# Four graph layers on one core: the order of the first graphs, the place of the exact arm, and the costs of a list planner

## The chip, the core and the metric

The kernel runs on one core of a Trainium2 chip. The metric is the device time of one execution in microseconds; lower is better. The engines are called as in the profile: PE (TensorE's matmuls, with PEld for its weight loads), DVE (VectorE), ACT (ScalarE), POOL (GpSimd) and SP (SyncE, which here issues all the DMAs).

## The reference, cut to what matters

The input is 32 graphs of 512 nodes with 128 features each, and one 512 x 512 matrix `adj` that all graphs share. Four layers follow one another; each normalizes, applies ReLU, and adds its result to x.

```python
h = relu(layernorm(x)); x = x + L0(h, adj)   # messages weighted by sigmoid scores
h = relu(layernorm(x)); x = x + L1(h, adj)   # five GRU steps
h = relu(layernorm(x)); x = x + L2(h, adj)   # adj @ (h @ weight) + bias
h = relu(layernorm(x)); x = x + L3(h, adj)   # Chebyshev sum, powers 0 to 3 of adj

# L0
x_h = elu(h @ Wi + bi)
e = sigmoid(a_tgt[:, :, None] + a_src[:, None, :] + be)      # a_src, a_tgt = x_h @ We, two halves
e = e * (adj + 0.005 * (1 - (adj != 0)))
recv = elu(concat([e @ x_h, x_h * e.sum(-1, keepdims=True)]) @ Wn + bn)
out = concat([recv, x_h]) @ Wm + bm

# L1, five times
m = adj @ h                                                  # both matrices are adj here
z = sigmoid(concat([m, m]) @ w3.T + h @ u3.T + biases)
r = sigmoid(concat([m, m]) @ w4.T + h @ u3.T + biases)
c = tanh(concat([m, m]) @ w5.T + (r * h) @ u5.T + biases)
h = (1 - z) * h + z * c
```

Here `adj` holds only zeros and ones, which matters for the kernel: a 0/1 matrix is unchanged when it is rounded to the one-pass matmul format.

## The kernel before, in words

**Staging.** The graphs go in groups of four. A graph's x is 512 x 128, kept on chip as 128 partitions x 512 columns. Nearly every operation works on one such 128x512 tile. A full fp32 product of that size takes TensorE several passes. A product with `adj` takes one pass for each part: when the matrix is exact in the one-pass format, the other operand is split into a high and a low part (`parts`, ACT L739 and DVE L743), and two one-pass products give the result (L769 in layers 1 and 2, L859 in layer 3). So the program has two arms: the exact one, and one with full fp32 products. A test of `adj` decides at run time: DVE L472 compares each rounded part with the original and sums the differences, PE L479 adds up over the partitions, DVE L484 writes the integer `inexact`, and each engine loads it (L906) and branches (L907). With this input the exact arm runs. Before the change the exact arm is the `else` of the branch, so the other arm's instructions stand between the branch and it.

**A list planner.** The instruction order is not written by hand. The kernel's Python lists operations with `op(engine, us, due, emit, reads, writes, ...)`: an assumed duration, a due time, and what it reads and writes. `Plan.order` then runs a list schedule: at each event, each engine takes of its ready operations the one that is due first, if its buffers are free. `result` is the assumed delay until others can use what was written; `known` computes it for a reader. Operations marked `two` (DVE with two operands in SBUF) and all POOL operations are not planned at the same time (`shared`). The order that comes out is emitted as it is, and every engine executes its own queue in that order. On the chip an engine starts an instruction when its semaphores allow, whatever the plan thought; what the plan fixes is the order.

The plan has two stretches: what is planned before `BRANCH` (30 us of planned time) comes ahead of the branch for both arms, and the rest is planned once for each arm. The due times come from `begin(b)`: graphs start `PACE` (56 us) apart, the first ones `FIRST_PACE` (10 us) apart, the last ones `LAST_PACE` apart.

**The first graphs.** Before the branch, SP loads graph 0, `Wi`, the four row blocks of `adj` (`A_nat`), small weights, then graphs 1 to 3. PE transposes graph 0's normalized tile (L334) and `adj` (L464, 16 transposes into four PSUM buffers). ACT rounds the transposed `adj` to `A_r` (L466) and scales it (L468); DVE makes the score mask (L469) and the test (L472). Then layer 0 of graph 0 goes on: the `Wi` product (L405), elu (ACT L492, L410, L495, DVE L497, L499), the product with `W_tok` for messages and scores (L521), the spread of the target scores (L558), tanh (ACT L572), masking (DVE L575), aggregation (PE L583).

**Later graphs.** In layer 0 of graphs 4 to 31, the target scores go through DRAM: a small tile is written (`d`) and read back as one row spread to all partitions (L548, `f<-d`), and the sums over the four score tiles are made on POOL (L594, three additions a graph). POOL also takes the power for each normalization (L439) and adds two biases to x (L414). In layer 1 every step writes h to DRAM and reads it back transposed (`m<-f`, `f<-m`). DVE has the adds and the gate combinations (L794, L801, L811 to L815) and block transposes (L346).

**Buffers.** There are 36 `f` tiles, 8 PSUM banks `b`, 8 small `s` tiles, and a few of other kinds; a planned operation that writes a new value waits in the plan until one is free.

Of the kernel before, what the change touches and what calls it, by code (L numbers as in the profile page):

```python
# [38 lines left out]
class Plan:  # L39
# [7 lines left out]
    def __init__(self, slots, ahead, last):  # L47
# [3 lines left out]
        self.shared, self.now = 0.0, 0.0  # L51

    def op(self, eng, us, due, emit, reads=(), writes=(), two=False, keep=0, result=None):
# [4 lines left out]
        o = Op(eng, us, self.RESULT[eng] if result is None else result, emit, two, keep)  # L58
        for v in reads:
            o.before.add(v.writer)  # L60
# [37 lines left out]
    def known(self, o, to):  # L98

        own = {"PE": 0.0, "ACT": 0.13, "DVE": 0.13}  # L100
        return o.known - o.result + own[o.eng] if to.eng == o.eng in own else o.known

    def order(self, end=None):
# [9 lines left out]
        for i, o in enumerate(left):  # L113
            index[o] = i
            o.waits = sum(not b.begun for b in o.before)
            o.ready = max([0.0, *(self.known(b, o) for b in o.before if b.begun)])
# [19 lines left out]
        while events:  # L136
# [3 lines left out]
            for e in self.until:  # L140
# [12 lines left out]
                for x in passed:  # L153
                    heapq.heappush(ready[e], x)
                if o is None:
                    continue
# [29 lines left out]
def tile_four_graph_layers(  # L186
# [35 lines left out]
    PACE, FIRST_PACE, LAST_PACE = 56.0, 10.0, 30.0  # L222
    BRANCH = 30.0
# [44 lines left out]
    op("DVE", 0.2, -9, lambda: nc.vector.memset(at(ones), 1.0), [], [ones])  # L268
    op("POOL", 0.2, -9, lambda: nc.gpsimd.memset(at(neg_half), -0.5), [], [neg_half])
# [8 lines left out]
    def load(v, src, due, us=0.5, to=None):  # L278
        op("SP", us, due, lambda: nc.sync.dma_start(at(v) if to is None else to(at(v)), src), [], [v])
        return v  # L280

    def load_const(src, shape, name, due, us=0.5):
        return load(const(name, shape), src, due, us)
# [10 lines left out]
    def load_graph(b, due):  # L294
        op("SP", 1.5, due, lambda: nc.sync.dma_start(
# [3 lines left out]
    load_graph(0, -9)  # L299
    Wi_sb = load_const(Wi, [P, P], "Wi_sb", -9)  # L300
    A_nat = [Val("f") for _ in range(NC)]
    for ic in range(NC):
        load(A_nat[ic], adj[ts(ic, P), :], -8, 1.3)
    bi_sb = load_column(bi, "bi_sb", -8)
# [6 lines left out]
    load_graph(1, -6)  # L311
# [3 lines left out]
    bm_bc = load_const(bm.partition_broadcast(P), [P, P], "bm_bc", -5)  # L315
    load_graph(2, -4)
    load_graph(3, -3)
# [107 lines left out]
    def layernorm(b, due):  # L425
# [13 lines left out]
        op("POOL", 1.2, due, lambda: nc.gpsimd.tensor_tensor(  # L439
# [19 lines left out]
    n_odd = const("n_odd", [P, NC])  # L459
    for jc in range(NC):  # L460
        pt, z, odd = Val("b"), Val("f"), Val("f")
# [3 lines left out]
        op("PE", T_TR, jc, turn, [*A_nat, ident], [pt])  # L465
# [480 lines left out]
```

## Time and profile before

| | |
|---|---|
| median of 3 runs | 1702.48 us (1700.79 to 1705.91) |
| the profiled execution's own time | 1704.23 us |
| its span, first to last instruction | 1702.4 us |
| mean granted TensorE clock | 0.996 |
| busy PE, DVE, ACT, POOL | 1665.6, 1478.8, 1099.6, 377.3 us |

The profile shows one execution. Busy time of PE is the union of its records, whose ends are modelled: dense matmuls overlap in it. The views used are the page (busy times, groups of instructions by line), the stretches (busy time of each engine in a window, with the granted clock), the timeline (instructions in order of time, neighbours of one kind merged, with the idle time before them and what ended it), the waits (who waited for whom in total), and the chain of waits that ended last. "issue" stands where the profile shows no reason for a wait.

### The profile page before, as it was taken

To read this page: it belongs to the slowest core of one execution; us is meant where nothing else is said; L and a number is where in the kernel's file an instruction comes from. 1 tells how busy PE (TensorE), PEld (TensorE's weight loads), DVE (VectorE), ACT (ScalarE), POOL (GpSimd) and SP (SyncE) were. 2 spreads that over 40 slices of the span, in tenths; PEclk is the share of its full clock that TensorE was granted. 3 is DMA by queue.
4 is the path that set the end of the run, shared out by engine and by line. 5 is a ranking of instruction groups with operands and counts; after the bars stand their busy time and mean duration, and the time that the engine had idled before them with its cause. 6 is when DMAs were issued, how large, how long until landed. Compare 5 with 4: busy or idle time off the path is not lost.

```text
span 1702.4 us, 21136 instructions
## 1 busy us (share of the span) xinstructions
PE 1665.6 (98%) x6521; PEld 1065.7 (63%) x6521; DVE 1478.8 (87%) x3325; ACT 1099.6 (65%) x2075; POOL 377.3 (22%) x301
## 2 busy tenths in 40 slices
PE   5999999999999999999999999999999999999998
PEld 3565555666666666665666665666666666666787
DVE  5789999999989998889989898899999888877842
ACT  5786767777666776566676666667576756655550
POOL 3231122312312222222212222122232221001210
PEclk8999999999999999999999999999999999999999
DMA  3122323253333332242333333333333323222302
GB/s 95 36 69 93 123 96 99 70 150 92 93 99 112 100 105 88 76 123 93 94 108 91 94 107 87 100 107 107 89 112 95 95 86 101 81 75 75 95 6 62
DMA packets 266873, 156.54 MB, mean 92 GB/s; under 512 B 75392, under 2 KB 235008, under 8 KB 266752
## 3 DMA queue, kind: packets, MB, share of 16 engines
q1 hardware_dynamic: 266752, 155.12, 30.9%
q8 instruction: 53, 0.87, 0.2%
q14 instruction: 68, 0.56, 0.1%
HBM read 82.25 MB, written 72.81 MB: 91 GB/s over the span
## 4 chain that ended last, share of the span: by engine, by line
PE 84%; DVE 8%; DMA 3%; ACT 3%; issue 2%; SPq 0%; POOL 0%; DVEq 0%; ACTq 0%; POOLq 0%
PE b L405 39%; PE b L769 18%; PE b L859 9%; PE b L850 6%; PE b L583 4%; PE b L619 3%; DMA f<-d 2%; PE b L521 2%; DVE f L575 2%; PE b L833 1%; DVE r L743 1%; PE b L606 1%; ACT f L447 1%; DVE f L794 1%; DVE f L346 1%
## 5 line engine op out<-in xcount | busy, mean ns | idle before, releaser
L394 ACT COPY f<-b 128x512 f32<-128x512 f32 x360 | 207.8, 585 | 151.6 <-PE b L769 105.8
L769 PE MATMUL b<-AQ,r 128*128 128x512 f32 x1024 | 304.4, 439 | 0.8 <-DVE r L743 0.8
L439 POOL TENSOR_TENSOR s<-s,nhalf 128x4 f32<-128x4 f32 x128 | 156.0, 1219 | 645.8 <-DVE s L437 610.1
L769 PEld LDWEIGHTS b<-AQ,r 128*128 128x128 f32 x1024 | 192.1, 188 | 90.5 <-issue 49.9
L794 DVE TENSOR_TENSOR f<-f,b 128x512 f32<-128x512 f32 x320 | 211.8, 677 | 20.4 <-PE b L405 16.5
L447 ACT ACTIVATE f<-x,s 128x128 f32<-128x128 f32 x512 | 210.1, 488 | 23.0 <-DVE s L442 22.7
L346 DVE STREAM_TRANSPOSE f<-f 128x512 f32<-128x512 f32 x244 | 204.6, 845 | 22.3 <-ACT f L447 21.7
L859 PE MATMUL b<-r,A_r 128*128 128x512 f32 x768 | 223.6, 426 | 0.0
L410 ACT ACTIVATE f<-f,b4w 128x512 f32<-128x512 f32 x160 | 115.4, 723 | 165.2 <-DVE f L794 164.7
L594 POOL TENSOR_TENSOR f<-f,f 128x512 f32<-128x512 f32 x84 | 130.9, 1559 | 307.3 <-DVE f L575 231.0
L405 PE MATMUL b<-f,u5T 128*128 128x512 f32 x320 | 163.9, 596 | 7.9 <-DVE f L801 7.8
L859 PEld LDWEIGHTS b<-r,A_r 128*128 128x128 f32 x768 | 139.0, 189 | 44.9 <-issue 23.0
L405 PE MATMUL b<-f,w4T 128*128 128x512 f32 x320 | 163.4, 593 | 0.2 <-ACT f L394 0.2
L405 PE MATMUL b<-f,u3T 128*128 128x512 f32 x320 | 163.0, 592 | 0.4 <-DMA f<-m 0.4
L405 PE MATMUL b<-f,w5T 128*128 128x512 f32 x320 | 162.8, 592 | 0.0
L405 PE MATMUL b<-f,w3T 128*128 128x512 f32 x320 | 162.5, 592 | 0.0
L769 PE MATMUL b<-A_r,r 128*128 128x512 f32 x512 | 151.8, 439 | 2.5 <-DVE r L743 2.5
L410 ACT ACTIVATE f<-b,b5w 128x512 f32<-128x512 f32 x160 | 109.2, 684 | 64.5 <-PE b L405 63.5
L743 DVE TENSOR_TENSOR r<-f,r 128x512 fp32r<-128x512 f32 x192 | 143.1, 749 | 8.2 <-ACT r L739 8.1
L850 PEld LDWEIGHTS b<-V,f 128*128 128x128 f32 x1024 | 130.5, 192 | 24.8 <-issue 20.6
L410 ACT ACTIVATE f<-f,b3w 128x512 f32<-128x512 f32 x160 | 115.2, 720 | 42.5 <-DVE f L794 41.6
L811 DVE TENSOR_TENSOR f<-f,f 128x512 f32<-128x512 f32 x160 | 114.7, 718 | 29.3 <-ACT f L410 28.7
(103 smaller groups left out, 2623.8 us busy)
## 6 DMA issues: line engine op xcount, KB each, us to landing
m<-f SPq DMA_DIRECT2D x244, 256.0 KB, 2.1
f<-m SPq DMA_DIRECT2D x184, 256.0 KB, 2.9
f<-m SPq DMA_DIRECT2D x240, 64.0 KB, 2.2
x<-in_x_dram SPq DMA_DIRECT2D x32, 256.0 KB, 3.1
out_dram<-x SPq DMA_DIRECT2D x32, 256.0 KB, 2.4
f<-d SPq DMA_DIRECT2D x28, 256.0 KB, 5.1
f<-in_adj_dram SPq DMA_DIRECT2D x4, 256.0 KB, 4.0
f<-in_L_gnn_weight_dram SPq DMA_DIRECT2D x2, 224.0 KB, 3.3
```

What stands on the lines that cost most here:

```text
L346: op("DVE", us, due, lambda: nc.vector.transpose(view_out(at(blocks)), view_in(at(src))), [src], [blocks])
L394: op("ACT", us, due, lambda: nc.scalar.copy(at(t), at(src)), [src], [t])
L405: nc.tensor.matmul(to, at(w), of, start=start, stop=stop)
L410: op("ACT", us, due, lambda: nc.scalar.activation(at(dst), at(src), AF.Tanh, bias=at(bias), scale=scale), [src, bias], [dst])
L439: op("POOL", 1.2, due, lambda: nc.gpsimd.tensor_tensor(stat(SCALE), stat(VAR), at(neg_half), op=ALU.pow), [s, neg_half], [s])
L447: nc.scalar.activation(at(h)[:, ts(c, P)], at(X[b])[:, c, :], AF.Relu, bias=stat(SHIFT)[:, c : c + 1], scale=stat(SCALE)[:, c : c + 1],)
L594: op("POOL", 1.4, d - 10, lambda: nc.gpsimd.tensor_tensor(at(dst), at(a), at(c), op=ALU.add), [a, c], [dst])
L743: op("DVE", T_VEC, due, lambda: nc.vector.tensor_tensor(part(lo), whole(), part(hi).bitcast(F32), op=ALU.subtract), [src, hi], [lo], two=two)
L769: nc.tensor.matmul(at(pa), at(part)[:, ts(jc, P)], view(at(columns)[:, jc, :]), start=jc == n == 0, stop=jc == NC - 1 and n == PARTS - 1,)
L794: op("DVE", T_VEC, d, lambda: nc.vector.tensor_tensor(at(s), at(u), at(pg), op=ALU.add), [u, pg], [s])
L850: nc.tensor.matmul(at(pz)[:, ts(i, D)], at(hT[i])[:, ts(ic, P)], at(V[k]), start=i == 0, stop=last and i == G - 1,)
L859: nc.tensor.matmul(at(pz), at(adjT)[:, jc, ts(ic, P)], at(part), start=False, stop=jc == NC - 1 and n == PARTS - 1,)
```

## The change

There are five edits.

1. *Loads.* Graph 1 is loaded right behind graph 0, `bi` ahead of `adj`, graph 2 right behind `adj`; `bm_bc` not before `BRANCH`. The planned cost of these issues goes from 1.5 and 1.3 us to 0.65.
2. *Test and preparation of `adj`.* The rounding for the test is made on the untransposed blocks (a new ACT copy into `short`, and the DVE comparison reads two SBUF tiles), so the test doesn't wait for the transposes. The transposes and `A_r` get later due times (8 and 22).
3. *Arms.* The condition is turned round, so that the exact arm follows the branch directly and the other arm stands behind it.
4. *Planner.* `BRANCH` 30 to 18, `FIRST_PACE` 10 to 14. Assumed costs: POOL power 1.2 to 1.35, POOL addition 1.4 to 1.6, the row read's result 3.6 to 5.0. In the arms, what another engine writes counts as known to PE 0.3 us later (`slack`). Before the branch, an operation is held when one with an earlier due time is about to be ready, and a planned operation may carry an earliest time.
5. *Dummies.* Ahead of the branch, wherever the plan leaves PE without work, it puts a matmul of `ones` with `ones` (128 x 128, planned at 0.224 us) into a PSUM bank that is set aside for it (`spare`) until the branch. There are 53 of them in the listing: 31 ahead of everything else, then 3, 15, 1 and 3 between the first operations.

```diff
+        if to.eng == o.eng in own:
+            return o.known - o.result + own[o.eng]
+        return o.known + (self.slack if to.eng == "PE" else 0.0)
...
+                if o is not None and end is not None and any(
+                    c.due < o.due and t < now + 0.3 * o.us for t, _, c in coming[e]
+                ):
+                    heapq.heappush(ready[e], (o.due, index[o], o))
+                    o = None
+                if o is None and e == "PE" and end is not None and self.idle.known <= now:
+                    order.append(self.idle)
+                    self.until[e] = now + self.idle.us
...
-    PACE, FIRST_PACE, LAST_PACE = 56.0, 10.0, 30.0
-    BRANCH = 30.0
+    PACE, FIRST_PACE, LAST_PACE = 56.0, 14.0, 30.0
+    BRANCH = 18.0
...
+    spare = places["b"].pop()
+    plan.free["b"].pop()
+    plan.idle = Op("PE", 0.224, 0.0, lambda: nc.tensor.matmul(
+        spare[:, :P], at(ones), at(ones), start=True, stop=True), False, 0)
+    plan.idle.known = 0.4
...
     load_graph(0, -9)
+    load_graph(1, -9)
     Wi_sb = load_const(Wi, [P, P], "Wi_sb", -9)
+    bi_sb = load_column(bi, "bi_sb", -9)
...
-        load(A_nat[ic], adj[ts(ic, P), :], -8, 1.3)
-    bi_sb = load_column(bi, "bi_sb", -8)
+        load(A_nat[ic], adj[ts(ic, P), :], -8, 0.65)
+    load_graph(2, -8)
...
-    bm_bc = load_const(bm.partition_broadcast(P), [P, P], "bm_bc", -5)
-    load_graph(2, -4)
-    load_graph(3, -3)
+    bm_bc = load_const(bm.partition_broadcast(P), [P, P], "bm_bc", -5, earliest=BRANCH)
+    load_graph(3, -6)
...
-        op("POOL", 1.2, due, lambda: nc.gpsimd.tensor_tensor(
+        op("POOL", 1.35, due, lambda: nc.gpsimd.tensor_tensor(
...
+    for ic in range(NC):
+        short, odd = Val("q"), Val("f")
+        op("ACT", T_COPY, 9, lambda ic=ic, short=short: nc.scalar.copy(
+            at(short), at(A_nat[ic])), [A_nat[ic]], [short])
+        op("DVE", 0.7, 9, lambda ic=ic, short=short, odd=odd: nc.vector.scalar_tensor_tensor(
+            at(odd), at(short).bitcast(F32), 1.0, at(A_nat[ic]),
+            op0=ALU.mult, op1=ALU.not_equal, accum_out=at(n_odd)[:, ic : ic + 1]),
+            [short, A_nat[ic]], [odd, n_odd], two=True)
...
-            op("SP", T_DMA, d, read, [row], [tgt], keep=KEEP, result=3.6)
+            op("SP", T_DMA, d, read, [row], [tgt], keep=KEEP, result=5.0)
...
-                op("POOL", 1.4, d - 10, lambda: nc.gpsimd.tensor_tensor(
+                op("POOL", 1.6, d - 10, lambda: nc.gpsimd.tensor_tensor(
...
+            plan.slack = 0.3
+            plan.free["b"].append((BRANCH, len(places["b"]) - 1))
...
-    with tc.If(taken > 0) as branch:
+    with tc.If(taken < 1) as branch:
+        arm(True)
+    with branch.Else():
         arm(False)
-    with branch.Else():
-        arm(True)
```

In the changed file the lines have moved: L394 becomes L417, L405 L428, L439 L462, L464 L495, L521 L548, L583 L610, L594 L621, L743 L773, L769 L799, L801 L831, L859 L889. The new lines that the steps name are L485 (ACT copy of `A_nat`), L487 (DVE test), L499 (ACT scaling of the transposed `adj`, before L468) and L288 (the dummies).

## The prediction

> **What bounds the kernel now.** I read the busy shares first, then the stretches of the first 50 us, then the waits of TensorE and the timeline around its longest ones. The first line says that TensorE (PE) is the bound and that little over 2% of the span can come back at all.
>
> ```profile
> PE 1665.6 (98%) x6521; PEld 1065.7 (63%) x6521; DVE 1478.8 (87%) x3325; ACT 1099.6 (65%) x2075; POOL 377.3 (22%) x301
> ```
>
> Busy PE is not yet work, since each record's end is modelled. So I price the records by their distance from start to start where the chain of waits shows them dense: 0.429 us for a 128x512 f32 record ("L405 x10" in 4.29), 0.2285 for a one-pass 128x512 (L769 and L859, 3.64 for 16 and 6.36 for 28), 0.112 for a 128-column f32 record (L850 x48 in 5.36), 0.109 for a transpose. With the counts of the groups: 2016 x 0.4288 + 2364 x 0.2285 + 2048 x 0.112 + 85 x 0.109 = 864.5 + 540.2 + 229.0 + 9.3 = 1643 us. The span is 1702.4, so 59.3 us are not work. Placed by start time, 27.1 of them lie in the first 50 us, 27.3 between 50 and 1650, and 4.9 at the end, where nearly all come after the last matmul (an addition, a store of 2.4 us to landing, the closing barrier).
>
> The first 50 us, by stretches (us, then busy us and records of PE, PEld, DVE, ACT, POOL, the granted clock, DMA):
>
> ```profile
> 0.00:10.00 10.00, 3.11 (x12) 2.50 (x13) 1.65 (x11) 4.31 (x9) 2.49 (x12) 1.00 0.69 194
> 10.00:20.00 10.00, 3.14 (x12) 2.06 (x10) 8.71 (x39) 5.47 (x10) 3.82 (x4) 0.80 0.19 55
> 20.00:30.00 10.00, 8.25 (x29) 5.08 (x30) 4.95 (x13) 7.63 (x18) 3.60 (x3) 0.52 0.16 47
> 30.00:40.00 10.00, 7.84 (x28) 4.03 (x27) 3.70 (x15) 5.33 (x12) 2.42 (x4) 1.00 0.43 108
> 40.00:50.00 10.00, 8.95 (x38) 5.25 (x37) 8.46 (x27) 8.99 (x22) 3.99 (x7) 1.00 0.00 0
> ...
> 8.31 3.62 PE L464 MATMUL b<-ident,f 128*128 128x128 f32 x16
> 20.61 2.10 PE L521 MATMUL b<-W_tok,f 128*128 128x130 f32 x8 [7.46 <-DVE f L499]
> 34.22 1.12 PE L583 MATMUL b<-f,f 128*128 128x512 f32 x2 [2.16 <-DVE f L499]
> ```
>
> Between 13 and 20 us DVE is full and PE waits 7.46 us for the first elu (DVE L499 of the file before); from 20 to 30 PE works at half clock. Then comes the branch. Here every engine jumps, because the exact arm is the second:
>
> ```profile
> L907 SPq COMPARE_BRANCH  x1: 45/45/45, 24.4 to 24.4; - x1
> L907 PEldq COMPARE_BRANCH  x1: 4549/4549/4549, 29.6 to 29.6; - x1
> ...
> 32.39 0.69 DVE L497 SCALAR_TENSOR_TENSOR f<-f,f 128x512 f32<-128x512 f32 x1 [4.03 <-issue]
> 33.05 0.40 POOL L751 CAST swap<-ident 128x128 fp32r<-128x128 f32 x1 [2.72 <-issue]
> ```
>
> SP's next instruction comes at 27.10, 2.7 us after its branch; PE's branch lasts 4.55 us, of which queued matmuls hide all but the 2.16 above. From 34.22 on PE is nearly full.
>
> In the middle PE waits for DVE, in a few pieces of over a microsecond:
>
> ```profile
> PE b L405 <- DVE f L801: 7.8, 7, 1.9
> PE b L769 <- DVE r L743: 3.3, 2, 2.5
> ...
> 1049.98 3.26 POOL L594 TENSOR_TENSOR f<-f,f 128x512 f32<-128x512 f32 x2 [0.69 <-DVE f L575]
> 1050.36 1.75 DVE L743 TENSOR_TENSOR r<-f,r 128x512 fp32r<-128x512 f32 x1
> 1052.04 1.76 DVE L815 SCALAR_TENSOR_TENSOR f<-f,f 128x512 f32<-128x512 f32 x1
> ...
> L594 POOL TENSOR_TENSOR f<-f,f 128x512 f32<-128x512 f32 x84 | 130.9, 1559 | 307.3 <-DVE f L575 231.0
> f<-d SPq DMA_DIRECT2D x28, 256.0 KB, 5.1
> ```
>
> The timeline shows a cause: while POOL adds (L594), a DVE instruction with two SBUF operands takes 1.75 us, not 0.685, and 5 us later PE loses 1.9 us on L801. In the whole trace 57 such instructions run over 1.0 us, 48 of them over an L594, and their excess is 53.5 us. The planner keeps the two apart but with 1.4 us for an addition that takes 1.56, and 3.6 for a row read that takes 5.1. From 50 to 1650 the waits whose end I can name cost PE about 15 us of the 27.3; the rest is handover between forms.
>
> **The change, part by part.** By the listings of the instructions, the exact arm has the same PE work as before (1643.1 us at the prices above) plus 53 dummy matmuls ahead of the branch. So everything is waits.
>
> *Start.* SP's queue now begins x0, x1, Wi, bi, then adj: the adj parts move back by two issues (0.95 us), to land at about 6.7 to 8.4 instead of 5.6 to 7.5 (issue to landing 4.0). PE meanwhile runs 31 dummies of 0.223 us from about 1.1. While the clock is half each takes 0.446. The change from half to full came 5.6 us after PE's first work in this trace (at 12.5; transposes at 0.213 each before it, 0.109 later), so I take 5 us: 11 dummies cold, 20 warm, end at 10.6 (9.7 to 11.4). That is 2 us after adj has landed, but it hides ACT's four new copies of A_nat (L485, 4 x 0.59) of which two stand ahead of x0's normalization, and DVE's test (4 x 0.69), which moves to plain adj. Then 16 transposes at 0.109 and x0's 4: 12.8; the copy L417 (0.59), three dummies; Wi (0.86) ends at 14.3; ACT's three scalings of the transposed adj (L499 of the changed file) are done at 14.9, then Exp, Tanh, Relu at 0.65 each to 16.9; DVE's two follow to 17.7. W_tok starts at 17.75 instead of 20.61. The last test, the count and the two masks of DVE bring `inexact` at about 20 instead of 23.5; graph 1's Wi comes at 21.2 instead of 26.33, graph 0's first aggregation (L610) at 23.2 instead of 28.20. The DMAs behind the branch (bm_bc, x4, then the weights) start at about 21 instead of 27; POOL's x + bm now waits for bm_bc there, and only the residual add much later reads it. By 23.2 PE has done 5.8 us of work: lost 17.4. Before, when PE was full at 34.22, 24.8 were lost, and 2.3 more by 50. With the same 2.3 after: 19.7 against 27.1, **7.5 us less** (4 to 10).
>
> *Branch.* Part of that 7.5 is 2.16 us of PE idle that goes if falling through is cheap. The trace shows no branch not taken. Bounds: 0.05 us (the instruction's own 45 ns on SP, ACT, POOL) and again 2.7 to 4.5. I take the low end, since the listed next instruction follows in line; the other end costs 1.5 to 2.3 us. The price comes back at the end: each engine now jumps over the other arm. SP's jump (2.7) starts after its last issue and lies beside the landing of 3.0; DVE's, if as long as its gap of 4.03, ends 0.5 us after the barrier did. I take **+0.5** (0 to 1.5). [...] The rows show 2.7 to 4.5, so I use them.
>
> *Clock.* [...] Here 16 transposes, with a piece of Wi behind them, filled the time before the grant at 12.5, so I charge nothing.
>
> *Costs in the list.* L594 at 1.6, L439 at 1.35 (measured 1.22, median 1.38), the row read at 5.0, 0.3 of slack for what PE reads, first graphs at 14 apart instead of 10. No instruction is added; the orders of all queues change. Bounds: nothing of the 15 us, all of it, or, with new collisions, a loss. PE now loses 15 for 53.5 us of stretching. If the right L594 price removes some two thirds (a POOL chain of three additions now slips by 3 x 0.16), PE gets about **9 us** back. I take that (-5 to +14).
>
> *Tail.* By the listing 95.9 us of PE work stand behind the last u5T product, 95.0 before, and no PE gaps lie there today: 0. SP's stores keep their order.
>
> Sum: -7.5 - 9 + 0.5 = -16. The profiled execution took 1704.23 (span 1702.4 and 1.8 around it), 1.75 above the median of the runs; I put the 16 to the median 1702.5: **1686.5 us**. About 0.3%, 5 us, is what can be told from no change.
>
> **Rivals.** *The middle keeps its waits:* the collisions only move, because POOL starts when DVE hands it data and not when planned. For it: L594 mostly waits for L575. Time: 1702.5 - 7 = 1695.5. *The start doesn't gain:* the dummies run cold to 14.9 (31 x 0.446) and the not-taken branch costs as much as the taken one. Against: the grant after 5.6 us. Time: -1 - 9 + 0.5: 1693. *The order is not what PE waited for in either place:* no change, 1702. *Slower:* in the middle, DVE at 93 to 99% from 150 to 450 us falls behind by new collisions. At 0.29 us of PE for each us stretched, it decides from 24 us more stretching (some 26 collisions) on, where the start's 7 us are gone; with 45 more, 1708. Against: POOL is given 84 x 0.2 + 128 x 0.15 = 36 us more room.
>
> **How the numbers follow.** The sum as told, 1678 to 1692: 0.60. Waits stay, to 1698: 0.20. Start fails, 1690 to 1698: 0.08. More than told, below 1678: 0.05. No change: 0.04. Slower: 0.03. The range 1677 to 1697 leaves out under 2 in 10.
>
> **What would show it.** Right: `inexact` near 20 us, the DVE and PE gaps at the branch gone, the full clock before 10 us and kept, PE full from about 24, lost work at 50 us near 20; stretched DVE instructions down from 57 to about 20, L801's waits below 3 us. Wrong: a half clock after 12 us, a gap of 2 us or more behind the branch, 50 or more stretched instructions, PE gaps after 1600, or an end more than 6 us after the last matmul.

## The result, and the profile after

The changed kernel takes 1696.03 us (median of 6 runs, 1693.68 to 1697.62) against 1703.74 for the kernel before (6 runs, 1700.79 to 1705.97): a ratio of 0.9954, with a 95% interval of 0.9943 to 0.9966. That is 7.7 us less. The forecast was 16 less; the time lies inside its range (1677 to 1697), but only just.

The profiled execution of the changed kernel took 1695.31 us, with a span of 1693.5. By the prediction's prices its PE work is again 1643.1 us (the dummies are not counted), so 50.4 us of the span are not work, against 59.3. By place, with PE's records sorted by their start ("middle" is from 50 to 1600 us in all that follows):

| not work, us | 0 to 50 | 50 to 1600 | 1600 to the end |
|---|---|---|---|
| before | 27.1 | 27.0 | 5.2 |
| after | 15.9 | 27.0 | 7.5 |
| step of the sum | -7.5 | -9 | +0.5 |
| measured | -11.2 | 0.0 | +2.3 |

So the start brought more than forecast, the end cost more, and the whole error is the middle. The lines of the page that answer to those shown of before (busy engines, the group of POOL's additions, the row read):

```profile
PE 1671.6 (99%) x6627; PEld 1075.1 (63%) x6627; DVE 1484.5 (88%) x3325; ACT 1100.3 (65%) x2079; POOL 381.7 (23%) x301
...
L621 POOL TENSOR_TENSOR f<-f,f 128x512 f32<-128x512 f32 x84 | 131.4, 1565 | 230.1 <-DVE f L602 159.2
...
f<-d SPq DMA_DIRECT2D x28, 256.0 KB, 5.4
```

PE is fuller on paper, but its 106 records more (6627 against 6521) are the two records of each of the 53 dummies. POOL's additions and the row read last about as long as before (1565 ns against 1559, 5.4 us against 5.1); only the planner's opinion of them changed.

The stretches of the first 50 us of the kernel after, and the start in its timeline:

```profile
0.00:10.00 10.00, 8.96 (x64) 8.96 (x65) 3.99 (x25) 4.86 (x10) 3.23 (x11) 1.00 0.76 226
10.00:20.00 10.00, 10.00 (x91) 9.37 (x89) 8.00 (x32) 8.31 (x18) 2.22 (x4) 1.00 0.08 20
20.00:30.00 10.00, 9.36 (x34) 4.67 (x33) 8.02 (x26) 9.02 (x21) 6.73 (x10) 1.00 0.55 150
30.00:40.00 10.00, 10.00 (x33) 5.08 (x32) 6.95 (x19) 10.00 (x24) 3.35 (x3) 1.00 0.01 3
...
1.04 8.97 PE L288 MATMUL b<-ones 128*128 128x128 f32 x62 [1.04 <-DVE ones L283]
9.85 1.47 PE L495 MATMUL b<-ident,f 128*128 128x128 f32 x12
16.91 1.06 PE L548 MATMUL b<-W_tok,f 128*128 128x130 f32 x8
18.77 0.14 DVE L511 CAST inexact<-b 1x1 int32<-1x1 f32 x1
21.70 3.70 PE L610 MATMUL b<-f,f 128*128 128x512 f32 x8 [0.64 <-DVE f L602]
```

The column of the granted clock is 1.00 in every stretch, where before had 0.80 and 0.52. It leaves out the time ahead of the first grant: until 4.81 us a dummy's record takes 0.213 us from start to start, behind it 0.112. The 7.46 us wait ahead of W_tok is filled, and 0.64 us is all that PE waits behind the branch. From 22 us on PE is full.

PE's longest waits in the kernel after:

```profile
PE b L799 <- DVE r L773: 4.5, 3, 2.5
PE b L428 <- DVE f L831: 3.1, 7, 0.8
PE b L428 <- ACT f L417: 2.5, 4, 1.1
```

The 7.8 us of before's L801 (now L831) are down to 3.1, as hoped; the split of the operands (L773) has 4.5 instead of 3.3, and ACT's copies (L417, before L394) have 2.5 instead of 1.4. Two-operand DVE instructions of over 1.0 us number 65 instead of 57, and their excess is 64.0 us instead of 53.5.

### The profile page after: what moved, and what is told of

Read it like the earlier page. It is cut to its first block, busy times and chain, and to the rows that moved or that the text cites. A ratio compares the mean times of both kernels' runs of the same rounds, so it can differ in the third digit from the quotient of the medians.

```text
span 1693.5 us, 21347 instructions
## 1 busy us (share of the span) xinstructions
PE 1671.6 (99%) x6627; PEld 1075.1 (63%) x6627; DVE 1484.5 (88%) x3325; ACT 1100.3 (65%) x2079; POOL 381.7 (23%) x301
## 4 chain that ended last, share of the span: by engine, by line
PE 77%; DVE 15%; ACT 4%; issue 2%; DMA 2%; SPq 0%; DVEq 0%; ACTq 0%
PE b L428 35%; PE b L799 16%; PE b L889 9%; PE b L880 5%; PE b L610 3%; PE b L646 3%; DVE f L602 2%; DVE r L773 2%; DVE f L369 2%; DVE f L824 2%; PE b L548 1%; PE b L863 1%; DVE f L841 1%; DVE f L831 1%; ACT f L470 1%
## 5 line engine op out<-in xcount | busy, mean ns | idle before, releaser
L417 ACT COPY f<-b 128x512 f32<-128x512 f32 x360 | 208.2, 586 | 168.2 <-PE b L799 114.8
L799 PE MATMUL b<-AQ,r 128*128 128x512 f32 x1024 | 300.2, 435 | 4.5 <-DVE r L773 4.5
L462 POOL TENSOR_TENSOR s<-s,nhalf 128x4 f32<-128x4 f32 x128 | 155.5, 1215 | 629.2 <-DVE s L460 610.6
L799 PEld LDWEIGHTS b<-AQ,r 128*128 128x128 f32 x1024 | 191.9, 188 | 93.1 <-issue 45.0
L824 DVE TENSOR_TENSOR f<-f,b 128x512 f32<-128x512 f32 x320 | 210.7, 673 | 30.5 <-PE b L428 23.6
L889 PE MATMUL b<-r,A_r 128*128 128x512 f32 x768 | 218.5, 421 | 0.0
L621 POOL TENSOR_TENSOR f<-f,f 128x512 f32<-128x512 f32 x84 | 131.4, 1565 | 230.1 <-DVE f L602 159.2
L428 PE MATMUL b<-f,u5T 128*128 128x512 f32 x320 | 164.0, 596 | 3.5 <-DVE f L831 3.1
L889 PEld LDWEIGHTS b<-r,A_r 128*128 128x128 f32 x768 | 139.5, 189 | 43.3 <-issue 20.1
L428 PE MATMUL b<-f,w4T 128*128 128x512 f32 x320 | 163.4, 593 | 2.5 <-ACT f L417 2.5
L428 PE MATMUL b<-f,w5T 128*128 128x512 f32 x320 | 162.9, 592 | 0.0
L428 PE MATMUL b<-f,u3T 128*128 128x512 f32 x320 | 162.6, 592 | 0.0
L428 PE MATMUL b<-f,w3T 128*128 128x512 f32 x320 | 162.3, 592 | 0.0
L773 DVE TENSOR_TENSOR r<-f,r 128x512 fp32r<-128x512 f32 x192 | 143.9, 753 | 10.8 <-ACT r L769 10.6
L799 PE MATMUL b<-A_r,r 128*128 128x512 f32 x512 | 151.8, 438 | 0.0
L841 DVE TENSOR_TENSOR f<-f,f 128x512 f32<-128x512 f32 x160 | 113.1, 709 | 29.4 <-ACT f L433 28.8
```

What stands on the lines that cost most here:

```text
L417: op("ACT", us, due, lambda: nc.scalar.copy(at(t), at(src)), [src], [t])
L428: nc.tensor.matmul(to, at(w), of, start=start, stop=stop)
L462: op("POOL", 1.35, due, lambda: nc.gpsimd.tensor_tensor(stat(SCALE), stat(VAR), at(neg_half), op=ALU.pow), [s, neg_half], [s])
L621: op("POOL", 1.6, d - 10, lambda: nc.gpsimd.tensor_tensor(at(dst), at(a), at(c), op=ALU.add), [a, c], [dst])
L773: op("DVE", T_VEC, due, lambda: nc.vector.tensor_tensor(part(lo), whole(), part(hi).bitcast(F32), op=ALU.subtract), [src, hi], [lo], two=two)
L799: nc.tensor.matmul(at(pa), at(part)[:, ts(jc, P)], view(at(columns)[:, jc, :]), start=jc == n == 0, stop=jc == NC - 1 and n == PARTS - 1,)
```

## The experiments

Each kernel's ratio is to runs of the kernel before on the same chip. The median of before lay between 1703.74 and 1706.28 us on these chips, so times are compared by their ratios where a few us matter (0.0010 is 1.7 us). "Stretch" is the number and excess of the two-operand DVE instructions over 1.0 us. Start, middle and end are the three columns above, each from one execution.

| kernel | median us | ratio (95%) | start | middle | end | stretch |
|---|---|---|---|---|---|---|
| b_list | 1699.87 | 0.9962 (0.9948 to 0.9977) | 26.7 | 24.6 | 5.1 | 51, 51.0 |
| a_start | 1714.59 | 1.0043 (1.0027 to 1.0059) | 18.4 | 40.4 | 7.6 | 60, 59.0 |
| a_start10 | 1708.41 | 1.0025 (1.0015 to 1.0034) | 21.5 | 34.8 | 7.1 | 64, 63.4 |
| a_pace10 | 1698.59 | 0.9960 (0.9948 to 0.9973) | 21.1 | 25.0 | 7.6 | 56, 55.3 |
| a_read | 1698.85 | 0.9966 (0.9951 to 0.9982) | 20.2 | 27.1 | 7.3 | 49, 49.0 |
| a_pool | 1699.90 | 0.9982 (0.9970 to 0.9993) | 15.9 | 31.3 | 7.4 | 51, 50.4 |
| a_noslack | 1695.50 | 0.9941 (0.9922 to 0.9961) | 17.1 | 27.6 | 7.4 | 56, 58.9 |
| a_slack | 1704.98 | 0.9993 (0.9981 to 1.0006) | 20.6 | 33.7 | 6.2 | 59, 57.9 |
| a_arms | 1696.96 | 0.9946 (0.9932 to 0.9961) | 21.0 | 25.5 | 5.2 | 60, 60.4 |
| a_nodummy | 1694.82 | 0.9933 (0.9918 to 0.9948) | 17.6 | 23.5 | 7.2 | 61, 59.2 |
| a_swap | 1694.24 | 0.9937 (0.9919 to 0.9955) | 16.7 | 25.7 | 7.0 | 60, 58.1 |
| a_noadd | 1676.69 | 0.9831 (0.9807 to 0.9854) | 16.7 | 8.4 | 7.2 | 12, 10.2 |
| a_stub | 1716.14 | 1.0071 (1.0051 to 1.0092) | 16.3 | 45.1 | 8.4 | 78, 77.1 |
| a_last | 1684.43 | 0.9883 (0.9869 to 0.9898) | 15.9 | 16.5 | 7.1 | 26, 24.3 |
| b_last | 1719.96 | 1.0096 (1.0082 to 1.0110) | 25.4 | 42.1 | 5.1 | 57, 53.7 |
| b_lastlist | 1694.70 | 0.9944 (0.9927 to 0.9960) | 28.8 | 15.6 | 5.1 | 33, 30.5 |
| a_lastold | 1689.64 | 0.9909 (0.9889 to 0.9928) | 20.6 | 17.9 | 6.2 | 35, 33.6 |

Experiments named b_ are edits of the kernel before, those named a_ of the changed one.

**The change in two halves.** b_list puts the planner's costs alone into the kernel before; a_start is the changed kernel with the old costs.

```diff
 b_list (before + these; a_start is the changed kernel with these undone)
-        op("POOL", 1.2, due, ...          # the power
+        op("POOL", 1.35, due, ...
-            op("SP", ..., result=3.6)     # the row read
+            op("SP", ..., result=5.0)
-                op("POOL", 1.4, d - 10, ...   # an addition of the score sums
+                op("POOL", 1.6, d - 10, ...
+            plan.slack = 0.3
```

> The kernel before with the planner's edits alone: POOL power 1.35, POOL addition 1.6, row read 5.0, and 0.3 us of slack for PE in the arms. Theory A (a corrected price cannot part POOL and DVE, because on the chip POOL starts when its data is there and not when the plan says): not-work of PE at the start stays 27, from 50 to 1650 us it stays 27 +-4, the end 5; time within 4 us of before; still 50 or more stretched DVE instructions. Theory B (the prediction: the prices part them, and in the changed kernel something else ate the gain): 50 to 1650 us falls by about 9, time 1694, stretched DVE instructions about 20.

> The changed kernel with the planner's old prices (1.2, 1.4, 3.6) and no slack, so with the start, the dummies and the arms alone. Theory A: as fast as the changed kernel within 3 us, about 1694 to 1697: the start's 11 us less 2.4 at the end. Theory B: slower than the changed kernel by the 9 us that the prices should give, 1703 or so.

The two halves don't add. By the ratios, the costs bring 6.5 us on the old start and 15 on the new one; the start, with the arms, costs 7 us with the old costs, and with the new ones the 1.4 us that it brings (3.8 by the medians) are hardly more than two measurements of one kernel differ by (a_swap, below). b_list fits theory A in the middle and in its stretching; a_start missed both of its expectations. In the profiles the new start does save 8.7 us of the first 50 us with the old costs, but the middle then loses 13.4.

What theory A says of POOL is shown directly. In all fourteen profiles with the additions in their old place, whether the plan has them at 1.4 or at 1.6, the first of a graph's three starts 0.08 to 0.5 us after the end of the second mask (typically 0.13), while DVE still has two masks to go.

The waits of PE in a_start, and one of its longest in the timeline:

```profile
PE b L610 <- DVE f L602: 8.3, 9, 2.8
PE b L428 <- DVE f L831: 8.0, 7, 2.0
...
995.64 0.45 SPq L575 DMA_DIRECT2D f<-d  x1
999.35 1.02 PE L428 MATMUL b<-f,w5T 128*128 128x512 f32 x2
1001.64 2.56 ACT L599 ACTIVATE f<-f,s 128x512 f32<-128x512 f32 x4 [3.04 <-DMA f<-d]
1002.40 3.59 DVE L602 SCALAR_TENSOR_TENSOR f<-f,mask 128x512 f32<-128x512 f32 x4 [3.07 <-ACT f L599]
1003.14 2.07 PE L610 MATMUL b<-f,f 128*128 128x512 f32 x3 [2.77 <-DVE f L602]
```

The row read is issued at 995.64, and ACT can begin its tanh 6.0 us later, where the plan had put it 3.6 us later. ACT, DVE and PE stand still one behind the other, 3.04, 3.07 and 2.77 us, in queues whose order was made for the shorter read. The changed kernel has no wait for L602 in the middle. So one part of what the costs are for is shown directly, and it was not in the prediction's sum, which priced POOL's addition only.

**Which cost.** Each kernel is the changed one with only some of the four values new.

```diff
 a_read:    row read 5.0; POOL 1.2 and 1.4, slack 0
 a_pool:    POOL 1.35 and 1.6; row read 3.6, slack 0
 a_noslack: both prices new; slack 0
 a_slack:   slack 0.3; all three prices old
```

> The changed kernel with one of its three prices alone: the row read at 5.0; POOL at 1.2 and 1.4, no slack. With old prices and no slack, PE lost 7.5 us to DVE's masks (L602), which hang on the row read; with all three prices 0.3. Theory R (the read's price is what counts): not-work from 50 to 1650 us near 27, L602's waits at most 1 us, time 1695 to 1699. Theory Q (POOL's prices count): near 40, 1708 to 1714.

> The changed kernel with POOL's new prices (1.35, 1.6) alone: the row read at 3.6 again, no slack. The complement of the kernel with the read's price alone. If the read's price is all that the prices bring: not-work from 50 to 1650 us near 40, DVE's masks (L602) again among PE's first waits with 4 us or more, 1708 to 1714. If each of the two would do: near 27, 1695 to 1699.

> The changed kernel with the new prices but without the 0.3 us of slack for PE. Theory S (the slack alone is what kept the middle at 27 us of not-work instead of the 40 of the kernel with old prices and no slack): 50 to 1650 us near 40, time 1707 to 1714. Theory P (the prices did it): near 27, time within 3 us of the changed kernel.

> The changed kernel with the slack but with the old prices (1.2, 1.4, 3.6). Theory S: 50 to 1650 us stays near 27, within 3 us of the changed kernel. Theory P: near 40, 1707 to 1714. If both this and the kernel without slack come out near 27, or both near 40, the two work together or the middle depends on the plan by chance.

The middle is 40.4 with none, 33.7 with slack alone, 31.3 with POOL's prices alone, 27.1 with the read alone, 27.6 with POOL's and the read's and 27.0 with all. The read alone gives all of it in the profile; POOL's prices alone give most of it. Beside both, the slack gives nothing (1695.50 and 1696.03). PE's waits for the mask in the middle go with the read's price: 7.1 us in a_start, 2.6 in a_pool, 0.9 in a_read, 0.2 in a_noslack. a_slack and a_pool came out between their expectations. Each of the three costs alone takes 7 to 13 of the 13.4 us away, so part of a_start's 40.4 may be the chance of one bad plan; the only run that plans it anew with its costs kept is a_start10, below. The stretch doesn't follow the middle at all: a_start has 59.0 us of it with 40.4 lost, the changed kernel 64.0 with 27.0.

**The spacing of the first graphs.**

```diff
 a_pace10: the changed kernel;  a_start10: a_start
-    PACE, FIRST_PACE, LAST_PACE = 56.0, 14.0, 30.0
+    PACE, FIRST_PACE, LAST_PACE = 56.0, 10.0, 30.0
```

> The changed kernel with the first graphs 10 apart again instead of 14. If the wider start made the middle worse (with old prices the new start has 40 us of not-work there, the old start 27), the stretch from 50 to 500 us falls from 13.5 to about 9 to 11 and the time by 2 to 5 us. If the spacing doesn't matter: within 2 us.

> The changed kernel's start with old prices, no slack, and the first graphs 10 apart as before. With 14 apart the middle has 40 us of not-work, the kernel before has 27 with the same prices. If the spacing is what exposed the row reads: 27 to 30, 1697 to 1701, L602's waits at most 2 us. If it is the other edits of the start (the branch at 18 of planned time, the loads): near 40, 1708 to 1714.

With the new costs the spacing changes the start from 15.9 to 21.1 (a PE gap of 3.58 us up to 24.75, and a half clock from 25.98 on) and the middle from 27.0 to 25.0; from 50 to 500 us more is lost and not less, 16.4 for 13.5, so the expected gain missed. With the old costs it takes the middle from 40.4 to 34.8, still far above before's 27.0. So 14 in place of 10 explains some 6 of the 13 us that the new start loses in the middle. What makes the rest isn't settled. By all kernels with the additions in their old place, five plans with the read at 3.6 lose 27.0, 31.3, 33.7, 34.8 and 40.4 us in the middle, and seven with it at 5.0 lose 23.5 to 27.6. The kernel before is the best of the first kind, and the only one of the five with the old start. Its order fits a chip that its costs didn't describe; whether by luck, or because the old start hides the read, isn't shown.

**The parts of the start.**

```diff
 a_arms: the arms in their old places
-    with tc.If(taken < 1) as branch:
-        arm(True)
-    with branch.Else():
+    with tc.If(taken > 0) as branch:
         arm(False)
+    with branch.Else():
+        arm(True)
 a_nodummy: no dummy matmuls
-    plan.idle.known = 0.4
+    plan.idle.known = 1e9
```

> The changed kernel with the arms in their old places, so that the exact arm is reached by a jump again and its end falls through. If the jump at the end is what made the end 2.4 us longer, the time from the last DVE addition to the end goes back from 6.9 to about 4.5 us, and the start shows gaps of 2.7 to 4.5 us on all engines near 20 us, of which PE feels 2 to 3: net -1 to +2 us. If the end is longer for another reason (the store that took 1.40 us to issue), the end stays near 6.9 and the whole is 2 to 3 us slower.

> The changed kernel without the 53 dummy matmuls (their PSUM bank stays set aside). If the warm clock is what the dummies bring: transposes at 0.21 us again, half clock for most of the first 25 us, not-work of PE in the first 50 us from 15.9 (dummies counted as not-work) to about 20, 4 us slower than the changed kernel. If the order alone made the start shorter: within 1 us, or 1 us faster, since adj lands at about 8.4 and the dummies end at 9.9.

The branch instruction in the kernel after (SP and PE; the shortest of the two is the branch itself, the other the jump over the second arm at the end; for SP the time behind that jump is not in its own 49 ns), and PE's in a_arms:

```profile
L937 SPq COMPARE_BRANCH  x2: 46/48/49, 19.8 to 1688.7; - x2
L937 PEldq COMPARE_BRANCH  x2: 92/1831/3570, 20.4 to 1682.0; - x2
```

```profile
L937 PEldq COMPARE_BRANCH  x1: 3746/3746/3746, 21.4 to 21.4; - x1
```

Falling through costs PE 92 ns; taking it, 3746, with a gap of 3.49 us in PE's work. a_arms has 5.1 us more lost in the start and 2.3 less at the end, so the place of the arms is worth 2.8 us in the profiles; the times (1696.96 and 1696.03) don't part the two. The dummies are worth 1.7 us of the start at most, although without them the clock isn't full. The stretches of a_nodummy:

```profile
10.00:20.00 10.00, 6.84 (x36) 5.51 (x35) 7.70 (x29) 7.46 (x16) 1.84 (x3) 0.77 0.06 14
20.00:30.00 10.00, 9.42 (x31) 4.69 (x30) 8.40 (x26) 8.55 (x18) 7.40 (x10) 0.89 0.53 145
```

PE is busy for only 6.84 us of the second ten: it waits for its operands there, and there the half clock costs little (17.6 us lost in the start, against 15.9). Its time is no worse (1694.82). So of the 11.2 us in the start, dummies and arms carry 1.7 and 5.1, if these add. The rest wasn't taken apart: the order of loads, test and masks is in it, but also the spacing and POOL's prices (see the start, below).

**How far two plans of one kind differ.** a_swap exchanges two lines.

```diff
-            add(sums[0], es[0], es[1])
             add(sums[1], es[2], es[3])
+            add(sums[0], es[0], es[1])
```

> The changed kernel with POOL's additions in another order: es[2]+es[3] first, then es[0]+es[1]. POOL then starts behind DVE's last mask (L602) instead of behind the second. In the changed kernel 25 of the 65 stretched DVE instructions are L602 over POOL's first addition, 26.6 of 64 us. If the collisions are set by when POOL's data is there, L602's stretching goes to below 5 us. If stretched DVE time is what makes PE wait (12.9 us of PE idle for 64), not-work in the middle falls by some 5 us, 1690 to 1692; if the slack covers such delays, the time stays within 2 us.

The planner takes what is ready first, and the order of the instructions on every engine stayed the same. So this is a second measurement of the changed kernel, and its expectations were not tested: 1694.24 us, 25.7 in the middle, 16.7 in the start. Differences of 2 us in time, of 3 by the ratios (0.9937 and 0.9954) and of 1.3 in a column are not read as effects here; this holds for the times of a_noslack and a_arms against the changed kernel, and a_nodummy (0.9933) is hardly beyond it.

**What POOL's additions cost.** a_noadd leaves the three additions out, for the score sums of graphs 4 to 31. a_stub makes them, but nobody reads their sum.

```diff
 a_noadd
-            add(sums[0], es[0], es[1])
-            add(sums[1], es[2], es[3])
-            add(sums[0], sums[0], sums[1])
+            sums[0] = es[0]
 a_stub: the high copy and the low subtraction read es[0] instead of sums[0]
```

> The changed kernel without POOL's 84 additions: the sum over the score tiles is left out for graphs 4 to 31, and the first tile stands in its place. An upper bound for what POOL's additions cost: stretched DVE time falls from 64 to about 12 us (the bias additions stay). If collisions are behind PE's waits in the middle, its not-work falls from 27 to about 17, 1685 to 1688. If the waits come from the order itself, it stays at 22 or more.

> The changed kernel with POOL's 84 additions still executed, but nobody waits for them: the high and low parts are taken from the first score tile, so the sum is left out for graphs 4 to 31. It parts two effects of the additions: their collisions with DVE stay, their delay (three in a row, some 5 us, ahead of the row sums) goes. If the collisions cost PE the 18 us by which the middle fell when the additions were left out, not-work in the middle stays at 22 or more, 1690 to 1695. If the delay does, it falls to 8 to 12, 1677 to 1682.

Without the additions 8.4 us are lost in the middle and 12 instructions are stretched: with all that hangs on them, the plan's order too, the additions cost PE some 18 us. PE's waits in a_noadd and in a_stub:

```profile
PE b L797 <- DVE r L771: 1.7, 1, 1.7
```

```profile
PE b L633 <- DVE q L628: 11.0, 12, 2.8
PE b L428 <- DVE f L636: 9.6, 9, 2.3
```

In a_stub nobody waits for POOL's sum any more, and the middle is the worst of all, 45.1, with 78 stretched instructions. So the loss doesn't need the time that the sums take to arrive. With the low subtraction (L628) freed to go earlier, 8 of its 28 fall under an addition and take 1.75 us (none does in the changed kernel). L636, for which PE waits 9.6 us, is not held itself; it comes late. a_stub moves other instructions too, so its 45.1 is no measure of the collisions alone.

**POOL's first addition put behind the last mask.**

```diff
 a_last: the changed kernel; b_last: the same in before (addition at 1.4)
-            def add(dst, a, c):
+            def add(dst, a, c, after=()):
                 op("POOL", 1.6, d - 10, lambda: nc.gpsimd.tensor_tensor(
-                    at(dst), at(a), at(c), op=ALU.add), [a, c], [dst])
-            add(sums[0], es[0], es[1])
+                    at(dst), at(a), at(c), op=ALU.add), [a, c, *after], [dst])
             add(sums[1], es[2], es[3])
+            add(sums[0], es[0], es[1], [es[3]])
             add(sums[0], sums[0], sums[1])
 b_lastlist: b_last with b_list's costs;  a_lastold: a_last with POOL's prices at 1.2 and 1.4
```

> The changed kernel with POOL's additions so that the first one is es[2]+es[3], and the second is planned behind the last mask as well: POOL starts when DVE's four masks (L602) are through. L602's stretching over the first addition, 24 to 27 us in the two profiles of the changed order, should go to below 5 us, the sums come some 1.5 us later. If stretched DVE time makes PE wait, not-work in the middle falls by 4 to 8 us, 1687 to 1691. If the additions then only meet other DVE instructions, the total of stretching stays above 50 us, and the time within 3 us.

> The kernel before with one edit, POOL's first addition planned and executed behind DVE's last mask (es[2]+es[3] first), at the old price of 1.4. In the changed kernel the same edit took stretched DVE time from 64 to 24 us, not-work in the middle from 27 to 16.5. If the collision is a matter of when POOL's data is there, and not of the start or the prices: stretching from 53 to about 25, the middle from 27 to 16 to 20, 1693 to 1698. If it needed the new prices: middle at 24 or more, within 3 us of before.

> The kernel before with POOL's additions behind the last mask and with the planner's edits (prices 1.35, 1.6, 5.0, slack 0.3). With the old prices the same order of additions made the middle worse (42 us of not-work; the collisions left the masks and met other instructions, 54 us of stretching in all). If price and place work only together (the plan knows when POOL starts, and how long it takes): stretching about 25, the middle 16 to 20, 1690 to 1696. If it was the new start that made the place pay: stretching 45 or more, the middle 30 or more, 1705 or more.

> The changed kernel with POOL's additions behind the last mask, but with POOL's old prices (1.2 and 1.4); row read 5.0 and slack stay. If the right price is what lets the plan keep DVE clear of additions whose start it knows: stretching back to 45 to 55 us, the middle from 16.5 to 28 or more, 1696 to 1705. If the place alone does it: stretching about 25 and 1684 to 1688.

The same graph's masks and additions in the timelines of the changed kernel and of a_last:

```profile
98.54 2.38 DVE L602 SCALAR_TENSOR_TENSOR f<-f,mask 128x512 f32<-128x512 f32 x2
98.17 1.61 POOL L621 TENSOR_TENSOR f<-f,f 128x512 f32<-128x512 f32 x1 [14.85 <-DVE f L602]
101.00 2.63 POOL L621 TENSOR_TENSOR f<-f,f 128x512 f32<-128x512 f32 x2 [1.23 <-DVE f L602]
```

```profile
98.44 1.28 DVE L602 SCALAR_TENSOR_TENSOR f<-f,mask 128x512 f32<-128x512 f32 x2
99.87 4.26 POOL L621 TENSOR_TENSOR f<-f,f 128x512 f32<-128x512 f32 x3 [2.88 <-DVE f L602]
```

In the changed kernel POOL adds as soon as two masks are done, at 98.17, while DVE has two to go: those take 2.38 us instead of 1.28. In a_last all three additions come behind the last mask at 99.87, and end at 104.13 against 103.63: the sum is half a microsecond later and DVE is 1.2 us earlier. Over all graphs, by the mask's group in the kernel after and in a_last:

```profile
L602 DVE SCALAR_TENSOR_TENSOR f<-f,mask 128x512 f32<-128x512 f32 x128 | 108.1, 894 | 7.0 <-ACT f L599 6.8
```

```profile
L602 DVE SCALAR_TENSOR_TENSOR f<-f,mask 128x512 f32<-128x512 f32 x128 | 81.6, 693 | 5.5 <-ACT f L599 5.3
```

No mask is stretched any more (mean 693 ns against 894). The whole stretch falls from 64.0 to 24.3 us, the middle from 27.0 to 16.5, and the time to 1684.43: 11.6 us less than the changed kernel (12 by the ratios), and faster than both. That is about the gain that the prediction had put on the prices, and by the same mechanism.

In the kernel before the same edit does harm (1719.96). The lines of b_last around its longest wait:

```profile
217.32 1.76 DVE L743 TENSOR_TENSOR r<-f,r 128x512 fp32r<-128x512 f32 x1
219.01 1.75 DVE L813 SCALAR_TENSOR_TENSOR f<-f,f 128x512 f32<-128x512 f32 x1
220.68 1.75 DVE L801 SCALAR_TENSOR_TENSOR f<-f,f 128x512 f32<-128x512 f32 x1
216.94 4.94 POOL L594 TENSOR_TENSOR f<-f,f 128x512 f32<-128x512 f32 x3 [4.21 <-issue]
222.48 2.07 PE L405 MATMUL b<-f,u5T 128*128 128x512 f32 x2 [2.90 <-DVE f L801]
```

The masks are clear (one of 128 is held), but three additions in a row lie over three instructions of the GRU chain, and PE waits 2.90 us for the last. The stretch is 53.7 us, as it was before, and PE loses 15 us more, outside both expectations. So the sum of held time doesn't set the loss; in these lines the instruction that is held is one that PE waits for. With the new costs (b_lastlist) the same place gives 15.6 in the middle. So place and costs work as a pair there. But POOL's own prices are not the half that counts: a_lastold, with 1.2 and 1.4, the read at 5.0 and the slack, still has 17.9 in the middle and 1689.64 us. Its expectation from the pair of place and POOL price, 28 or more, missed. POOL's prices add 1.4 us of the middle to that (some 5 us in time, most of it in the start, 20.6 to 15.9). The read's price, with the slack, is then what makes the place work. This is put together from two starts: no run has the place with all the old costs on the new start, and the slack wasn't taken away separately.

## Why the prediction was right or wrong, point by point

**Start: right in kind, too small (-11.2 for -7.5).** The clock was full 3.8 us after the first dummy, where I took 5; the dummies ended at 9.85 (10.6 forecast), W_tok began at 16.91 (17.75), `inexact` came at 18.77 (20), graph 1's Wi at 20.03 (21.2), the aggregation L610 at 21.70 (23.2). All steps came in the order told, each about a microsecond early. How soon the clock is full differs from run to run: in a_swap, with the same instructions in the same order, it came 5.4 us after the first dummy, and over all kernels with these dummies after 2.9 (a_start) to 6.1 us (a_noslack). The other part is the 2.3 us that I carried over from before for the time up to 50 us: in this execution hardly anything is lost there. That isn't the new start alone: the other kernels with it have 15.9 to 21.5. Six of them (a_start, a_start10, a_pace10, a_read, a_slack, a_lastold) have one PE gap of 2.2 to 3.6 us that ends between 24.7 and 29.3 us, all but a_start with a half clock for 3.41 us, and all six have POOL's old prices or the old spacing. Three pairs differ in POOL's prices alone: the start is 18.4 and 15.9 (a_start, a_pool), 20.2 and 17.1 (a_read, a_noslack), 20.6 and 15.9 (a_lastold, a_last). So these prices pay 2.5 to 4.7 us in the start, where the sum gave them nothing.

**Branch: right.** Not taken it costs PE 0.092 us and SP 0.046, the low end that I chose, and 0.64 us is left of the gap of 2.16. The taken branch costs PE 3746 ns in a_arms.

**End: mis-sized (+2.3 for +0.5).** The end of the kernel after: the last additions, SP's stores, and SP's first instructions in the closing barrier:

```profile
1685.38 1.88 DVE L901 TENSOR_TENSOR x<-x,b 128x512 f32<-128x512 f32 x3 [5.50 <-PE b L889]
1686.10 2.55 SPq L906 DMA_DIRECT2D out_dram<-x  x3
...
L971 SPq DRAIN  x3: 7/7/13, 1692.7 to 1693.0; - x3
```

SP finishes its last issue at 1688.65 and takes the jump at 1688.7. In the trace its next instruction comes at 1692.18, 3.5 us later, where I had taken 2.7. The stores themselves end later too, since three take 2.55 us to issue, not 1.57. The jump lies beside the landing, as told, but is longer than it: from the end of the last addition to the end of the span it is 6.25 us instead of 3.89. In a_arms it is 3.87.

**Clock: right.** The clock did not fall behind the dummies, with 20 transposes in between (1.00 in every stretch up to 50 us), so there was nothing to charge. With dummies ahead and between, this trace can't tell whether it would have come to full with transposes alone ahead of it, but a_nodummy can:

```profile
6.69 1.03 PE L495 MATMUL b<-ident,f 128*128 128x128 f32 x2 [6.69 <-DMA f<-in_adj_dram]
...
11.77 0.75 PE L495 MATMUL b<-ident,f 128*128 128x128 f32 x4
12.65 1.13 PE L428 MATMUL b<-f,Wi_sb 128*128 128x512 f32 x2
```

Its first 20 records on PE are all transposes. From 9.21 us they come 0.213 us apart up to 11.98, and 0.110 from 12.13 on, so the full clock was granted between the two, ahead of the first product at 12.65. Here the full clock came with nothing but transposes ahead of it on PE.

**Costs in the list: the step that failed (0 for -9).** Two assumptions of it fell. First, "the right L594 price removes some two thirds" of the stretching: there was more of it, 65 instructions and 64.0 us (51 and 51.0 with the prices and slack alone, b_list). POOL's first addition starts when DVE hands it its second mask, whatever its price; what a_last took away by making it wait for the last one is what the price could not. 25 of the 65 are masks under that addition. Second, I added the middle's gain to the start's as if the new start left the middle alone. It doesn't: with the old costs, the new start makes the middle 13.4 us worse (27.0 to 40.4), and the costs then bring just that back (40.4 to 27.0, a_start to the changed kernel). What makes the new start so dear there is settled for the spacing alone, some 6 us. The zero of the middle is the difference of these two. My own line, that the orders of all queues change, should have had a price.

**The rivals.** "The middle keeps its waits" (1695.5, at 0.20) named the right cause, POOL starting when it is handed data, and nearly the right time. It is half of the story, since it saw no loss from the start, and that its time came so near is in part luck: the start brought 3.7 us more than it took, and the end cost 1.8 more. a_start and b_last are slower than before, 1714.59 and 1719.96, but not as "Slower" has it, by more stretching: theirs (59.0 and 53.7) is close to before's, so 0.29 us of PE for each us stretched is not a rate to count with.

**What I had named as signs.** `inexact` near 20, the clock, the branch and PE full from about 24 came out right; "down to about 20" stretched instructions came out wrong; L801's waits ended at 3.1 where I asked for under 3; an end more than 6 us after the last matmul, which I had named as a sign of a wrong step, is there: 7.3 us, from 1686.25 to 1693.5.

## What to carry to other kernels

Don't add up the gains of edits to a planned order: replan with each alone and with both, since an order that fits the chip can be lost by any edit (here the start alone cost 7 us by its ratio, and with the new costs it cost nothing). A planner's cost can keep two engines apart only if the engine that is to start later really waits until then; where the chip starts as soon as data is there (POOL here, 0.08 to 0.5 us behind the second mask), put the wanted order into the data dependences (here some 12 us with the new costs; with the old ones, in the kernel before, it cost 16). Price first what a whole chain waits for, such as a read that comes back through DRAM, and judge a collision by who waits for the instruction held, not by the total of held time.

## What the runs showed of the hardware that I had not expected

- DVE instructions with two SBUF operands are held while POOL adds 128x512 f32 tiles. In the kernel after, the 52 stretched ones that start beside a running addition take 1.75 us in the median (1.02 to 1.80) instead of 0.685, and all end 0.54 to 0.55 us behind it, whenever they started (0.03 to 0.99 us after its start): these rows show no sharing but a wait for the addition's end. Ten more that start beside an addition take 0.67 to 0.68 us: five in its last 0.06 us, and five beside two additions that began while such a DVE instruction ran and that last 2.86 and 3.48 us themselves. The 84 additions of 1.57 us cost this PE-bound kernel some 18 us of 1693 (the middle is 27.0 with them and 8.4 in a_noadd). The additions pay too: the 13 that meet no such DVE instruction take 1.27 to 1.30 us, so the measured time that the planner's new price copies has the collision in it.
- A taken jump costs SP 3.5 us at the end of the changed kernel and PE 3.7 ahead of the exact arm in a_arms, and one not taken 0.092 on PE and 0.046 on SP in the changed kernel.
- A single PE gap in the middle of full work sometimes brings a half clock for 3.41 us and sometimes not: after gaps of 1.89 us (b_list, at 318.9), 1.91 (a_pool, at 1092.7) and 2.50 (a_swap, at 309.2) it fell, after 2.50 (the changed kernel, at 309.3) and 2.51 (before, at 429.8) it did not. The changed kernel and a_swap have the same instructions in the same order there. The mean granted clocks go with it: 0.994 in b_list against 0.996 in before, 0.998 in a_pool and a_swap against 0.999 in the changed kernel. No run here shows what decides it.
- A DRAM row read to all partitions (256 KB written) lands after 5.1 us before and 5.4 after (medians of 28), while the other 256 KB moves of the steady state take 2.1 to 3.3.
